# First layer of a two-layer kernel: chunk 1 loaded in halves, ten matmuls on zeros, and padded rows for the first batch's mask, W and x

## The chip, the cores and the metric

The kernel runs on one core of one Trainium2 chip. The metric is the device time of one execution in microseconds (us), lower is better. A core has TensorE (PE; its weight loads are shown as PEld), VectorE (DVE), ScalarE (ACT), GpSimd (POOL) and SyncE (SP), which here only issues transfers. Sixteen DMA engines move data between the chip's memory (HBM) and the on-chip memory.

## The reference, cut to what matters

There are 8 batches of 256 rows and 1024 features, all in float32. Two layers follow each other, each with a residual:

```python
# layer 0, for each batch b
y = x[b] + x[b] @ W.T + bias + coeff[b] * (x[b] @ (2 * mask[b] - 1))
# layer 1
out[b] = y + y @ weight[ids[b]].T
```

mask is (8, 1024, 1024) of int32 zeros and ones, W is (1024, 1024), weight is (8, 1024, 1024), and ids picks one of the 8 weights for each batch.

## The kernel before, in words

**Layer 0 as one product.** The mask of a batch is turned into a weight: ScalarE computes 2c * mask - c in place ("scale"), VectorE adds W transposed ("fold"), and TensorE multiplies x by the result. Layer 1 multiplies y by the chosen weight.

**Stages.** There are 16 stages: layer 0 and layer 1 of 8 batches. All but the first are computed as a two by two block product with seven block multiplications (p1 to p7, in the order p1, p5, p6, p2, p7, p3, p4) instead of eight. That costs VectorE sums of blocks of x (s1 to s4, line L542) and of weight blocks (t1 to t4, line L559). In this first block stage, which is layer 1 of batch 0, t1 is block 12 minus 11, t2 is 22 minus t1, t3 is 22 minus 12, and t4 is 21 minus t2. p5 needs s1 and t1, p6 needs s2 and t2, p7 needs s3 and t3. Its matmuls are L598; those of all later stages are L608. Results are gathered by L672.

**The first stage is done plainly**, because everything waits for the first data. Its 1024 input features are 8 chunks of 128 (k = 0 to 7). A chunk has a mask row block (`mask0`, loaded on L283), a W row block (`w0T`, L287, into `w0_sb`) and a slice of x (`x0T`, L274). A whole chunk of mask or of W is 128 partitions by 1024 numbers, 512 KB. The list `pieces` holds what is loaded at once: before, chunk 0 in two halves of 512 columns and chunks 1 to 7 whole. Each piece has a load of the mask, a load of W, a scale (`scale_first`, ACT L301), a fold (`fold_first`, DVE L309) and its matmuls (`mm_first`, PE L316: two records of the profile to one call, 16 to a chunk). `parts` cuts scale and fold of a piece into smaller instructions: the first piece by 256 columns and piece 2, which is chunk 1, by 512. x comes in three loads that `load_w0` issues behind pieces 0, 2 and 3: for chunks 0 and 1 (256 KB), 2 and 3 (256 KB) and 4 to 7 (512 KB). The results are evicted with bias and residual by `evict_first` (DVE L343), in four instructions, two for each half of the outputs.

**The order.** Work is described as tasks with an engine, an estimated length, their inputs and a latest time. `plan` simulates the engines with these estimates and emits tasks by planned start, so each engine's order is fixed at build time and each engine then runs strictly in its order. All loads are issued by SP in one queue. The framework gives DMAs eight completion semaphores in rotation, so a load is not issued before the one eight places ahead of it has landed; the coefficients' load, issued by ACT, takes the first of them. Weight and mask buffers (11 of 1 MB) come free when their last user is done.

**Before the first data.** TensorE runs eight matmuls of bfloat16 zeros, 512 columns each (L806), and among them, after the fifth, one that spreads the 8 coefficients over all partitions (L808). VectorE makes the two scale factors from it (L809, L810), and ScalarE's first scale waits for them.

Of the kernel before, what the change touches and what calls it, by code (L numbers as in the profile page):

```python
# [14 lines left out]
P = 128  # L15
Q = 32
BLOCKS = ("11", "12", "22", "21")
WBUFS = 11


PRODUCTS = {
# [120 lines left out]
def kernel(  # L142
# [26 lines left out]
    nc = tc.nc  # L169
    B = coeff.shape[1]  # L170
    _, _, _, KH, TH = xT.shape
    NL, _, _, _, H = w1T.shape
    KC, D = 2 * KH, 2 * H
# [4 lines left out]
        for name, bufs in (  # L178
            ("const", 1),
            ("w", WBUFS),  # L180
            ("a", 3),
# [8 lines left out]
    )  # L190
    room = {"w": WBUFS, "a": 3, "r": 3, "turn": 2, "s1": 2, "u2": 2, "ps": 8}
    shapes = {
# [16 lines left out]
    zeros = const.tile([P, H], BF16, name="zeros")  # L209
# [10 lines left out]
    def task(*args, **kw):  # L220
        tasks.append(Task(*args, **kw))
        return tasks[-1]

    def take(r: Buffer):
        count[0] += 1
        r.tile = pools[r.pool].tile(shapes[r.pool], F32, tag=r.pool, name=f"{r.pool}_{count[0]}")
        return r.tile
# [30 lines left out]
    first = {(j, h): Buffer("ps") for j in range(2) for h in range(2)}  # L258
    xb = Buffer("r")
    half = KH // 2  # L260
    pieces = [(0, ds(0, H)), (0, ds(H, H))] + [(k, ds(0, D)) for k in range(1, KC)]
    w0_rows = w0_sb.rearrange("p k j n -> p k (j n)")

    def x0_view():
        flat = x0.tile.rearrange("p q k n -> p (q k n)")[:, 0 : KC * 2 * TH]
        return flat.rearrange("p (k n) -> p k n", k=KC)
# [5 lines left out]
    def load_x0(lo: int, hi: int, queue):  # L272
        pairs = slice(lo // 2, hi // 2)
        queue.dma_start(  # L274
            out=x0_view()[:, lo:hi].rearrange("p (g k) n -> p g (k n)", k=2),
            in_=x0T[pairs].rearrange("g p n -> p g n"),
        )

    def load_mask(n: int):
        k, cols = pieces[n]  # L280
        if m[k // 2].tile is None:
            take(m[k // 2])
        nc.sync.dma_start(out=m_view(k)[:, cols].bitcast(I32), in_=mask0[k][:, cols])  # L283

    def load_w0(n: int):
        k, cols = pieces[n]
        nc.sync.dma_start(out=w0_rows[:, k, cols], in_=w0T[k][:, cols])  # L287
        if n in (0, 2, 3):
            load_x0(*{0: (0, 2), 2: (2, KH), 3: (KH, KC)}[n], nc.sync)

    def parts(n: int):

        k, cols = pieces[n]
        size = {0: 2 * P, 2: H}.get(n, cols.size)
        return k, [ds(at, size) for at in range(cols.start, cols.start + cols.size, size)]

    def scale_first(n: int):
        k, spans = parts(n)
        for cols in spans:
            t = m_view(k)[:, cols]  # L300
            nc.scalar.activation(  # L301
                t, t.bitcast(I32), AF.Identity, bias=cn_sb[:, 0:1], scale=c2_sb[:, 0:1]
            )

    def fold_first(n: int):
        k, spans = parts(n)
        for cols in spans:
            t = m_view(k)[:, cols]
            v.tensor_tensor(t, t, w0_rows[:, k, cols], ALU.add)  # L309
# [43 lines left out]
    for n, (k, cols) in enumerate(pieces):  # L353
        share = cols.size / D
        opens = opened != k // 2
        length = {0: 0.4, 2: 0.75}.get(n, 1.22 * share)
        ld = task(
            "DMA",
            1.32 * share,
            lambda n=n: load_mask(n),  # L360
            takes=[m[k // 2]] if opens else [],
            uses=[] if opens else [m[k // 2]],
            latency=1.5,
            latest=0.2 * n,
        )
        ld2 = task(
            "DMA", 1.32 * share, lambda n=n: load_w0(n), latency=1.5, latest=0.2 * n + 0.1
        )
        sc = task("ACT", length, lambda n=n: scale_first(n), after=[ld], uses=[m[k // 2]])
        fo = task("DVE", length, lambda n=n: fold_first(n), after=[sc, ld2], uses=[m[k // 2]])  # L370
        folded.append(fo)
        last_scale = sc
        opened = k // 2
        if n == 0:
            tasks[0].takes = [x0] + list(tasks[0].takes)
            tasks[0].uses = [x0] + list(tasks[0].uses)
            x0.users += 1
# [91 lines left out]
    def stage(s: int):  # L469
# [66 lines left out]
        def sum_of(what: str, after=()):  # L536
# [24 lines left out]
            for n, rows in enumerate(parts):  # L561
                t = task(
                    "DVE",
                    BLOCK / len(parts),
                    lambda rows=rows: emit(rows),
                    after=[done[left], done[right], done.get(what), *after],
                    takes=[W[what]] if fresh and n == 0 else [],
                    uses=src + ([W[what]] if fresh and n else []),
                )
                if fresh and n == 0:  # L570
                    t.stage = s
                done[what] = t
# [222 lines left out]
    with tc.manual_schedule():  # L795
        take(x0)
        nc.scalar.dma_start(out=c_row, in_=coeff)
        v.memset(zeros, 0.0)
        v.memset(ones, 1.0)
        v.memset(warm, 0.0)  # L800

        nc.scalar.activation(warm, warm, AF.Identity, bias=warm, scale=1.0)
        idle = pools["ps"].tile([P, H], F32, tag="ps", name="idle")
        c_ps = pools["ps"].tile([P, B], F32, tag="ps", name="c_ps")
        for n in range(8):
            nc.tensor.matmul(out=idle, lhsT=zeros[:, 0:P], rhs=zeros, start=True, stop=True)  # L806
            if n == 4:
                nc.tensor.matmul(out=c_ps, lhsT=ones, rhs=c_row, start=True, stop=True)  # L808
                v.tensor_scalar(c2_sb, c_ps, 2.0, None, ALU.mult)  # L809
                v.tensor_scalar(cn_sb, c_ps, -1.0, None, ALU.mult)  # L810
        for t in plan(tasks, room, may_take):
            t.emit()
            if t is folded[0]:

                v.memset(ids_sb, 0)
                v.memset(b_sb, 0.0)
                nc.gpsimd.dma_start(out=ids_sb, in_=ids)
                nc.gpsimd.dma_start(out=b_sb, in_=biasT)
# [58 lines left out]
```

## Time and profile before

| what | value |
|---|---|
| time, three runs | 403.77, 404.0, 405.08 us; median 404.0 |
| profiled execution | 404.47 us, span from the first to the last instruction 402.7 us |
| TensorE busy | 396.5 us, 98% of the span, 1154 records |
| VectorE busy | 330.5 us, 82% |
| ScalarE busy | 183.5 us, 46% |
| GpSimd busy | 27.2 us, 7% |
| moved by DMA | 102.99 MB, mean 256 GB/s; by SP's queue 87.23 MB |
| granted TensorE clock | 0.999 |

How to read the profile's lines. A line of the groups or the timeline names the engine, the source line, the operation, output and input tiles, shapes and count; in brackets stands how long the engine was idle before and what ended the wait. In the timeline the first number is the start in us from the span's start and the second the length. In the windows view each row is a stretch of time with the busy time of each engine asked for and, in brackets, its count of instructions, then the granted clock, the DMA engines' busy share and GB/s. In the list of waits, each line tells who waited for whom: total us, times, longest. In the chain, each step is followed back to what released it.

### The profile page before, as it was taken

What the parts mean: (1) busy time and instruction counts of PE and PEld (TensorE: products, weight loads), DVE (VectorE), ACT (ScalarE), POOL (GpSimd) and SP (SyncE); (2) the same over time, 40 slices, a digit from 0 to 9 for tenths busy, and PEclk for the clock granted to TensorE, in tenths of its full rate; (3) what the DMA queues carried; (4) which work ended last, traced back from release to release, by engine and by line L of the source; (5) the groups of instructions that cost most, each with busy time, mean ns of one, the idle gap of its engine ahead of it and who ended that gap; (6) DMA issues with size and microseconds to landing.
All of it is one profiled execution on the core that took longest, in us unless ns stands there. A gap on an engine that the chain in (4) does not pass through costs nothing.

```text
span 402.7 us, 3428 instructions
## 1 busy us (share of the span) xinstructions
PE 396.5 (98%) x1154; PEld 201.8 (50%) x1154; DVE 330.5 (82%) x306; ACT 183.5 (46%) x303; POOL 27.2 (7%) x44
## 2 busy tenths in 40 slices
PE   8899999999999999999999999999999999999996
PEld 5689995444444444444444444444444444444443
DVE  2347999999999999799968998789977999668242
ACT  3461735205952396880069610894119920391000
POOL 1000111100011100011010100102001020001101
PEclk9999999999999999999999999999999999999999
DMA  7999999982696828958399583987659694701102
GB/s 268 408 413 422 422 335 400 380 293 107 251 343 194 357 104 341 335 164 319 111 401 304 187 336 112 370 255 282 239 200 338 194 365 157 281 33 53 53 0 105
DMA packets 18564, 102.99 MB, mean 256 GB/s; under 512 B 2226, under 2 KB 2482, under 8 KB 9074
## 3 DMA queue, kind: packets, MB, share of 16 engines
q1 hardware_dynamic: 13952, 87.23, 55.9%
q0 software_dynamic: 4448, 15.47, 14.4%
q8 instruction: 9, 0.15, 0.1%
q14 instruction: 9, 0.07, 0.1%
q10 hardware_dynamic: 146, 0.07, 0.1%
HBM read 94.38 MB, written 8.39 MB: 255 GB/s over the span
## 4 chain that ended last, share of the span: by engine, by line
PE 92%; DMA 4%; DVE 2%; issue 1%; SPq 0%; DVEq 0%
PE ps L608 84%; PE ps L598 5%; DMA w_sb<-w0T 4%; PE ps L316 4%; DVE w L559 1%; DVE a L343 0%; DVE w L309 0%; SPq L283 0%; DVE a L542 0%; SPq L274 0%; SPq L287 0%; DVE r L757 0%; DVEq L343 0%; DVEq L309 0%
## 5 line engine op out<-in xcount | busy, mean ns | idle before, releaser
L608 PE MATMUL ps<-w,a 128*128 128x512 f32 (+1 forms) x792 | 336.7, 588 | 0.0
L608 PEld LDWEIGHTS ps<-w,a 128*128 128x128 f32 x792 | 149.9, 190 | 186.7 <-issue 183.4
L559 DVE TENSOR_TENSOR w<-w,w 128x2048 f32<-128x2048 f32 (+1 forms) x61 | 136.8, 2252 | 3.0 <-PE ps L608 2.5
L453 ACT ACTIVATE a<-turn 32x256 f32<-32x256 f32 x224 | 92.7, 414 | 68.5 <-DVE turn L439 65.7
L672 DVE TENSOR_TENSOR r<-r,ps 128x512 f32<-128x512 f32 x73 | 49.1, 680 | 24.9 <-PE ps L608 24.6
L529 DVE TENSOR_TENSOR w<-w,w_sb 128x2048 f32<-128x2048 f32 x28 | 63.9, 2286 | 5.7 <-ACT w L515 5.7
L515 ACT ACTIVATE w<-w,cn_sb,c_sb 128x2048 f32<-128x2048 int32 x28 | 58.5, 2091 | 15.7 <-DMA w<-mask 15.3
L542 DVE TENSOR_TENSOR a<-a 128x512 f32<-128x512 f32 x59 | 39.4, 686 | 0.3
L644 ACT ACTIVATE s<-ps 128x512 f32<-128x512 f32 x15 | 8.9, 591 | 63.2 <-PE ps L608 54.0
L316 PE MATMUL ps<-a,w 128*128 128x256 f32 x128 | 30.5, 399 | 1.1 <-DVE w L309 1.0
L698 POOL DMA_DIRECT2D out<-r x31 | 17.0, 550 | 190.1 <-DVE r L672 190.0
L316 PEld LDWEIGHTS ps<-a,w 128*128 128x128 f32 x128 | 25.3, 201 | 6.8 <-DVE w L309 3.2
L644 ACT ACTIVATE u<-ps 128x512 f32<-128x512 f32 x15 | 8.9, 595 | 39.2 <-PE ps L608 38.8
L309 DVE TENSOR_TENSOR w<-w,w_sb 128x1024 f32<-128x1024 f32 (+2 forms) x11 | 10.2, 934 | 15.2 <-DMA w_sb<-w0T 12.8
L598 PE MATMUL ps<-a,w 128*128 128x128 f32 x192 | 22.0, 276 | 0.2 <-DVE a L542 0.2
L598 PEld LDWEIGHTS ps<-a,w 128*128 128x128 f32 x192 | 21.8, 192 | 0.5 <-DVE a L542 0.4
L418 POOL DMA_DIRECT2D r<-bias x7 | 8.7, 1245 | 173.9 <-DMA r<-xR 173.9
L439 DVE STREAM_TRANSPOSE turn<-r 128x512 f32<-128x512 f32 x28 | 19.8, 708 | 0.6
L301 ACT ACTIVATE w<-w,cn_sb,c_sb 128x1024 f32<-128x1024 int32 (+2 forms) x11 | 10.9, 1004 | 14.6 <-DMA w<-mask 13.1
L672 DVE TENSOR_TENSOR r<-r,s 128x512 f32<-128x512 f32 x14 | 9.6, 684 | 6.6 <-ACT s L644 6.6
L672 DVE TENSOR_TENSOR r<-r,u 128x512 f32<-128x512 f32 x14 | 9.6, 686 | 3.4 <-ACT u L644 3.4
L343 DVE TENSOR_TENSOR a<-ps,r 128x512 f32<-128x512 f32 x4 | 2.7, 688 | 3.2 <-PE ps L316 3.2
(27 smaller groups left out, 24.8 us busy)
## 6 DMA issues: line engine op xcount, KB each, us to landing
w<-w1T SPq DMA_DIRECT2D x32, 1024.0 KB, 8.4
w<-mask SPq DMA_DIRECT2D x28, 1024.0 KB, 10.0
out<-r POOLq DMA_DIRECT2D x31, 256.0 KB, 7.4
r<-xR SPq DMA_DIRECT2D x7, 1024.0 KB, 8.0
a<-xT SPq DMA_DIRECT2D x7, 1024.0 KB, 9.2
r<-bias POOLq DMA_DIRECT2D x7, 1024.0 KB, 15.7
w<-mask SPq DMA_DIRECT2D x7, 512.0 KB, 9.9
w_sb<-w0T SPq DMA_DIRECT2D x7, 512.0 KB, 10.2
```

Source lines behind the costliest of these rows:

```text
L316: nc.tensor.matmul(out=t.rearrange("p (c n) -> p c n", c=half)[:, c % half], lhsT=m_view(k)[:, ts(oc, P)], rhs=x0_view()[:, k], start=k == ...
L439: lambda t=t, opens=not turned: v.transpose(out=(take(r) if opens else r.tile)[:, t], in_=view(source.tile)[:, 2 * t + j]),
L453: nc.scalar.activation(to[:, :, :, f], src[:, :, :, g], AF.Copy)
L515: nc.scalar.activation(t, t.bitcast(I32), AF.Identity, bias=cn_sb[:, b : b + 1], scale=c2_sb[:, b : b + 1])
L529: lambda q=q: v.tensor_tensor(W[q].tile, W[q].tile, w0[q], ALU.add),
L542: lambda: v.tensor_tensor(part(what), part(left), part(right), op),
L559: v.tensor_tensor(to[:, rows], a, c, op)
L598: nc.tensor.matmul(out=t[:, ts(c, TH)], lhsT=W[w].tile[:, k, ts(c, P)], rhs=part(a)[:, k], start=opens and c == 0 and k == 0, stop=k == KH ...
L608: nc.tensor.matmul(out=t[:, cols], lhsT=part(a)[:, k], rhs=W[w].tile[:, k, cols], start=opens and k == 0, stop=k == KH - 1, skip_group_che ...
L644: lambda: nc.scalar.activation(take(r), bank.tile, AF.Copy),
L672: v.tensor_tensor(to, left, get(r), op)
L698: lambda: (queue or nc.gpsimd).dma_start(out=out0[:, block(q)] if flipped else out[b - 1, :, int(q[0]) - 1, lo:hi], in_=R[b].tile[:, block ...
```

## The change

Five things change.

- `pieces`: chunk 1 is loaded, scaled and folded in two halves of 512 columns, as chunk 0 already is. There are now ten pieces, and chunks 2 to 7 are pieces 4 to 9.
- The loads of x follow pieces 0, 3 and 5: the second still comes behind chunk 1, and the third behind chunk 3 instead of chunk 2.
- `parts`, and the planner's length of it: the split of scale and fold into 512 columns goes from chunk 1, which is now halved anyway, to chunk 2.
- The zeros: after the eight matmuls of 512 columns come one of 256 and one of 128.
- `PAD`: each row of `w0T`, `x0T` and `mask0` in HBM gets 128 unused numbers (512 bytes) at its end. Rows of mask and W lie 4608 bytes apart instead of 4096, rows of x 2560 instead of 2048. The loads read the same numbers as before.

The planner runs with the new tasks, so the order changes elsewhere too. On SP only the loads named here differ up to the first weights. On VectorE, in the first block stage, t3 moves from before the last two evictions to behind s2 and one L672 sum; one weight fold of the next stage moves back by two instructions; and in later stages some weight sums, one s sum and two transposes move by a few places. Lines of the tile function from L277 on are two higher than before (L316 becomes L318, L598 L600), and those at the end a little more.

```diff
+PAD = 128
...
-    pieces = [(0, ds(0, H)), (0, ds(H, H))] + [(k, ds(0, D)) for k in range(1, KC)]
+    pieces = [(k, ds(j * H, H)) for k in range(2) for j in range(2)]
+    pieces += [(k, ds(0, D)) for k in range(2, KC)]
...
-            in_=x0T[pairs].rearrange("g p n -> p g n"),
+            in_=x0T[pairs, :, 0 : 4 * TH].rearrange("g p n -> p g n"),
...
         nc.sync.dma_start(out=w0_rows[:, k, cols], in_=w0T[k][:, cols])
-        if n in (0, 2, 3):
-            load_x0(*{0: (0, 2), 2: (2, KH), 3: (KH, KC)}[n], nc.sync)
+        if n in (0, 3, 5):
+            load_x0(*{0: (0, 2), 3: (2, KH), 5: (KH, KC)}[n], nc.sync)
...
-        size = {0: 2 * P, 2: H}.get(n, cols.size)
+        size = {0: 2 * P, 4: H}.get(n, cols.size)
...
-        length = {0: 0.4, 2: 0.75}.get(n, 1.22 * share)
+        length = {0: 0.4, 4: 0.75}.get(n, 1.22 * share)
...
-        for n in range(8):
-            nc.tensor.matmul(out=idle, lhsT=zeros[:, 0:P], rhs=zeros, start=True, stop=True)
+        for n, size in enumerate((H, H, H, H, H, H, H, H, 2 * P, P)):
+            nc.tensor.matmul(
+                out=idle[:, 0:size], lhsT=zeros[:, 0:P], rhs=zeros[:, 0:size], start=True, stop=True
+            )
...
+    for k in ("w0T", "x0T", "mask0"):
+        arrays[k] = np.pad(arrays[k], ((0, 0), (0, 0), (0, PAD)))
```

## The prediction, made before the changed kernel ran

> **What bounds the kernel now.** I read the chain of work that ended last, then what TensorE waited for, then TensorE's first 45 us in order of time, then the stretch that fills its gaps. The chain's shares and all of TensorE's waits:
>
> ```profile
> PE 92%; DMA 4%; DVE 2%; issue 1%; SPq 0%; DVEq 0%
> PE idle L806 <- DVE zeros L798: 1.2, 1, 1.2
> PE ps L316 <- DVE w L309: 1.0, 2, 0.8
> PE ps L598 <- DVE a L542: 0.2, 1, 0.2
> ```
>
> TensorE is the bound, and what it waits for lies in the first 41 us. From 40.83 on it has no gap, so a microsecond won before that is won at the end, if nobody else falls behind. The timeline of TensorE (start, length):
>
> ```profile
> 3.97 1.46 PE L806 MATMUL idle<-zeros 128*128 128x512 bf16 x3
> 5.49 5.54 PE L316 MATMUL ps<-a,w 128*128 128x256 f32 x16
> 11.81 7.50 PE L316 MATMUL ps<-a,w 128*128 128x256 f32 x32 [0.78 <-DVE w L309]
> 19.50 17.53 PE L316 MATMUL ps<-a,w 128*128 128x256 f32 x80 [0.19 <-DVE w L309]
> 36.87 3.73 PE L598 MATMUL ps<-a,w 128*128 128x128 f32 x32
> 40.83 4.40 PE L598 MATMUL ps<-a,w 128*128 128x128 f32 x37 [0.22 <-DVE a L542]
> ```
>
> A chunk is 16 records of L316. At full rate starts are 0.2155 us apart, so a chunk is 3.45; chunks 1 to 7 need 24.1 us. Chunk 0 begins at 5.49, chunk 1 at 11.81, 2 at 15.58, 3 at 19.50, and from there 80 records run without a wait to the next line at 36.87. The gaps shown understate the loss: they are counted after a modelled matmul end. By starts, chunk 3 comes 7.69 after chunk 1, where 6.90 would do. What feeds them, in the timelines of VectorE and ScalarE:
>
> ```profile
> 9.67 1.52 ACT L301 ACTIVATE w<-w,cn_sb,c_sb 128x512 f32<-128x512 int32 x2 [2.01 <-DMA w<-mask]
> 11.06 1.29 DVE L309 TENSOR_TENSOR w<-w,w_sb 128x512 f32<-128x512 f32 x2 [2.68 <-DMA w_sb<-w0T]
> 14.30 1.23 DVE L309 TENSOR_TENSOR w<-w,w_sb 128x1024 f32<-128x1024 f32 x1 [1.95 <-DMA w_sb<-w0T]
> 18.22 1.23 DVE L309 TENSOR_TENSOR w<-w,w_sb 128x1024 f32<-128x1024 f32 x1 [2.69 <-DMA w_sb<-w0T]
> 20.78 1.23 DVE L309 TENSOR_TENSOR w<-w,w_sb 128x1024 f32<-128x1024 f32 x1 [1.34 <-DMA w_sb<-w0T]
> ```
>
> Each fold waits for W's chunk. Chunk 3 arrives 3.9 us after chunk 2, later ones every 2.56: between them lie the 512 KB of x that load_w0 issues. From chunk 3 on arrivals outrun TensorE. The last stall is VectorE's own order:
>
> ```profile
> 32.82 0.69 DVE L343 TENSOR_TENSOR a<-ps,r 128x512 f32<-128x512 f32 x1 [3.03 <-PE ps L316]
> 34.29 4.55 DVE L559 TENSOR_TENSOR w<-w,w 128x1024 f32<-128x1024 f32 x3
> 38.76 1.28 DVE L343 TENSOR_TENSOR a<-ps,r 128x512 f32<-128x512 f32 x2
> 40.08 0.69 DVE L542 TENSOR_TENSOR a<-a 128x512 f32<-128x512 f32 x1
> ```
>
> The evictions at 38.76 could have started at 37; they stand behind a 2.29 us weight sum (t3, the third of the L559 row). s1 at 40.08 comes late and p5 starts at 40.83. By starts, p1 to p6 takes 7.63 us (36.87 to 44.50) where two products at 3.57 need 7.14: 0.49 lost.
>
> **Chunk 1 in halves.** The same bytes come as four loads of 256 KB instead of two of 512. The 1 MB of chunk 1 now lands half by 9.2 (midway between W's landings, 7.47 and 10.94). The first half's mask is there near 8.5, its scaling 0.81 puts it at 9.3, and the fold of 0.69 ends at 10.1. TensorE ends chunk 0 at 10.87 (last start 10.65 plus 0.22), so chunk 1 starts there, not at 11.81. The second half folds from about 11.2 to 11.9 (landing near 11.07, 0.69); TensorE wants it at 12.6. Chunk 1 is done at 14.3 to 14.4. The two added loads cost SP 0.42 us each while queued bytes cover it. SP's order now makes load 8 wait for the coefficients and 9 for the first mask (landed at 3.39); later waits are for loads in order, with over 2 MB issued ahead, so I cost the queue at nothing. Without that cover a late issue would cost its 0.42.
>
> 2 KB packets take 84 ns each in the trace's packet records, 4 KB ones 159 to 164: 32 x 84 against 16 x 160 ns per engine is 0.13 us later for everything behind.
>
> **What moves with the halves.** Chunk 2 takes over the split into 512 columns: W at 14.3 + 0.13, one fold of 0.69 instead of 1.23, so TensorE starts it at 15.17 instead of 15.58. It waits 0.8 there, and a first matmul after a wait costs 0.1 more. The 512 KB of x moves behind chunk 3, which lands 1.28 earlier: fold from 17.07 to 18.3, wanted at 18.75. So it no longer waits. Chunk 4 is where it was, plus 0.13: folded at 22.13, wanted at 22.2; x is there at 18.3. Hence 15.2 + 0.1 + 96 x 0.2155 = 35.99 for p1's start, against 36.87: **0.88 us**.
>
> The plan changes too. On VectorE t3 goes behind the evictions, s1, t2, s2 and one L672. With chunk 7 ended at 36.0, the two evictions (0.65 each in a row) and s1 end at 38.0, and p5 is wanted at 39.6: no stall, **0.49 us** more. t2 then ends at 40.3, s2 at 40.9 (p6 wants them at 43.1), t3 at 43.7 and s3 at 45 (p7 wants them at 50.3). Other moves after 60 us shift single weight sums or transposes by one or two places; in the trace the products they feed have 2.1 us to spare or more.
>
> **Zeros.** The last 512-wide one streams until 5.22; the new 256 and 128 columns at the half rate (0.213, 0.107) run to 5.54, so they fill the gap and delay the first real matmul by up to 0.08. Chunk 1's end moves to 14.4, under the 15.17 of chunk 2: nothing. On the clock, the windows of L316 (length, busy, count):
>
> ```profile
> 5.50:9.00 3.50, 3.50 (x8) 1.00 1.01 356
> 9.40:11.00 1.60, 1.60 (x8) 1.00 1.08 409
> ```
>
> Eight in 3.5 us, then eight in 1.6: starts are 0.427 apart until 9.04 and 0.2155 after 9.35, though the granted clock reads 1.00 throughout. The Trainium skill (TensorE: Matmul & The Clock Gate, Part 1) says half rate ends after about 3.4 us of sustained activity, in a free-running window. By the row it took 8 us from 1.20, with breaks at 3.3 to 4.0 (the coefficient matmul) and 5.2 to 5.5. By the rule, one break fewer may bring full rate at about 5.8, ending chunk 0 up to 1.7 earlier; but chunk 1's half is not there before 10.1 and chunk 2 not before 15.17, so by either the sum is unchanged. If full rate comes only at 11.9, chunk 0 ends at 12.3 and the 0.88 falls to about 0.2.
>
> **Rows 512 bytes longer.** Nothing in the trace shows it, so it is bounded. For a gain: the rates by window (last column GB/s) are
>
> ```profile
> 4.00:5.00 1.00, 1.00 (x4) 0.25 (x3) 0.26 (x3) 0.65 (x2) 0.00 (x0) 1.00 0.94 231
> 9.00:10.00 1.00, 1.00 (x5) 0.86 (x4) 0.00 (x0) 0.33 (x1) 0.00 (x0) 1.00 1.04 410
> 18.00:19.00 1.00, 1.00 (x7) 0.80 (x5) 0.78 (x1) 0.11 (x1) 0.00 (x0) 1.00 1.06 422
> ```
>
> Between 2 and 9 us packets take up to 1.65 us instead of 84 or 160 ns; that excess adds up to 1.0 us per engine, the most padding can win. Against it, full rows at the same pitch of 4 KB run at 401 to 422 GB/s from 9 on, and the slow packets include rows that lie end to end. The skill (DMA: Bandwidth & Descriptors, Latency and other measured facts) reports slow copies at power-of-two row pitches, but from 512 KB up, cured by 4 KB more and not by 192 bytes: by that rule a 512 byte pad at a pitch of 4 KB need not help. For a loss: chunks no longer lie in one piece; if the disturbed rate of the early windows became usual, a fifth (my estimate, 410 to 330 GB/s). I take zero, the row of the undisturbed packets.
>
> **Sum.** 0.88 + 0.49 = 1.37 us. The profiled execution took 404.47 (span 402.7, 1.77 around it), so 403.1; the median of the runs shown lies 0.47 lower: **402.6**.
>
> **VectorE as cover.** It is busy from 40 to 160 us but for 1.6. It waits once, 0.91 at 68.5 to 69.44, for p5 of the next stage. Its work from 34.29 to 68.53 is 34.24 us; starting when the weights land (33.45 + 0.13) it ends at 67.8, p5 at 67.9: it keeps pace. p1 of the stage at 110.44 needs ScalarE's turns, done at 109.42: 1.0 in hand.
>
> **Rivals.**
> A (0.42): as summed, 402.6; its own range 402.1 to 403.2.
> B (0.26), padding takes the early excess away: loads 1.0 earlier; chunk 2 starts at 14.4, when chunk 1 ends, and no chunk waits: 14.4 + 96 x 0.2155 = 35.1, gain 1.78 + 0.49 = 2.27: 401.7. For: the early windows. Against: the end-to-end rows.
> C (0.16), the gain is mostly hidden: chunk 4's fold later than 22.2, a late full rate, or VectorE behind at 110: 0.2 to 0.9 won, 403.4.
> D (0.16), slower: padded rows load slower. It decides at chunk 4: about 6.3 MB lie ahead of its fold, 15.4 us at 410 GB/s. At 9% slower (1.4 us) the gain is gone. At 20%, chunk 4 is folded at 25.2 to 25.9, up to 2.8 after its start now (23.1), and t1's weights come later still, so the 0.49 goes too: about 406.5. For: loads bound this stretch. Against: the packet durations of 9 us on look engine-bound, not memory-bound.
>
> **Numbers.** About 0.3% (1.2 us) is what a measurement of this kernel can tell from no change. A lies just beyond it: 0.62 of it is faster, the rest same. Faster 0.42 x 0.62 + 0.26 = 0.52; same 0.16 + 0.16 = 0.32; slower 0.16. From B's best (401.4) to the lower part of D (405.2), the range leaves out about 0.15.
>
> **What would show it.** Right: L318 (L316 before) with one wait near 15, none at 11.8 or 19.5; p1 (now L600) at 36.0; no wait for s1. B: 350 GB/s or more in the windows at 3 to 7. D: 4 KB packets over 175 ns, chunk 4's fold after 23.5. I am wrong if p1 starts after 36.6, or if a wait appears after 60.

## The result, and the profile after

| | before | changed |
|---|---|---|
| median of the runs | 404.2 us (403.77 to 405.08, 7 runs) | 402.53 us (401.9 to 402.92, 7 runs) |
| profiled execution | 404.47 us, span 402.7 | 402.53 us, span 400.8 |
| p1 starts (first block product) | 36.87 | 35.80 |
| p6 starts | 44.50 | 42.95 |

The ratio of the means is 0.9953, with an interval of 0.9942 to 0.9965. By medians that is 1.67 us less, by means 1.91, where 1.37 had been forecast (402.6).

The chain of work that ended last, as the changed kernel's page sums it by engine:

```profile
PE 95%; DMA 3%; SPq 0%; DVE 0%; issue 0%; DVEq 0%
```

TensorE's waits in the changed kernel (what it waited for and what ended the wait; total us, count, longest):

```profile
PE idle L808 <- DVE zeros L800: 1.2, 1, 1.2
PE ps L318 <- DVE b_sb L820: 0.3, 1, 0.3
```

VectorE's steps (a fold, the evictions, s1) are nearly gone from the chain. The waits for folds and for s1 are gone from the list; a new one of 0.3 stands ahead of the first real matmul. (The view names a setting of `b_sb` for it; the load of x landed at 5.93, just before the start at 6.06.) TensorE's timeline:

```profile
3.97 1.78 PE L808 MATMUL idle<-zeros 128*128 128x512 bf16 x5
6.06 29.90 PE L318 MATMUL ps<-a,w 128*128 128x256 f32 x128 [0.31 <-DVE b_sb L820]
35.80 9.43 PE L600 MATMUL ps<-a,w 128*128 128x128 f32 x83
```

The whole first stage is one row: 128 records with no wait that this view can show, and the block products join it without one. Looking at single starts, one short wait is left: chunk 1's last record starts at 14.48 and chunk 2's first at 14.90. From p6 on every product starts 1.55 or 1.56 us earlier than before, to the last stage; the remaining 0.35 of the difference in span lies behind the last matmul. There the last store lands 2.40 us after the start of that matmul instead of 2.62, and the program ends 1.16 after the landing instead of 1.29. So nothing was given back after 45 us, and 0.35 was won at a place that the forecast did not look at. VectorE, with what it waited for:

```profile
14.16 1.29 DVE L311 TENSOR_TENSOR w<-w,w_sb 128x512 f32<-128x512 f32 x2 [2.55 <-DMA w_sb<-w0T]
16.69 1.23 DVE L311 TENSOR_TENSOR w<-w,w_sb 128x1024 f32<-128x1024 f32 x1 [1.24 <-DMA w_sb<-w0T]
20.61 1.22 DVE L311 TENSOR_TENSOR w<-w,w_sb 128x1024 f32<-128x1024 f32 x1 [2.69 <-DMA w_sb<-w0T]
...
32.62 0.69 DVE L345 TENSOR_TENSOR a<-ps,r 128x512 f32<-128x512 f32 x1 [0.17 <-PE ps L318]
33.91 2.36 DVE L561 TENSOR_TENSOR w<-w,w 128x1024 f32<-128x1024 f32 x2 [0.60 <-DMA w<-w1T]
36.19 1.28 DVE L345 TENSOR_TENSOR a<-ps,r 128x512 f32<-128x512 f32 x2
37.51 0.69 DVE L544 TENSOR_TENSOR a<-a 128x512 f32<-128x512 f32 x1
38.12 2.28 DVE L561 TENSOR_TENSOR w<-w,w 128x2048 f32<-128x2048 f32 x1
```

Chunk 3 is folded at 16.69 instead of 18.22, and the long gap between arrivals has moved behind it, to chunk 4 (20.61), where TensorE still has work. The evictions at 36.19 follow t1 at once, s1 ends at 38.2, and p5, which wants it at 39.37, finds it there. The L561 row at 38.12 is t2.

The early loads look as before (windows of one us; last two columns the DMA engines' busy share and GB/s):

```profile
4.00:5.00 1.00, 1.00 (x4) 0.40 (x4) 0.25 (x3) 0.65 (x2) 0.00 (x0) 1.00 0.85 246
9.00:10.00 1.00, 1.00 (x5) 0.83 (x5) 0.42 (x1) 0.54 (x1) 0.00 (x0) 1.00 1.04 402
```

The packets' excess over 84 and 160 ns, per engine up to 10 us, is 1.2 us; before it was 1.1. So this one profile shows no effect of the padding on the early loads. The times of the experiments below say that the padding is worth something.

### The profile page after: what moved, and what is told of

Its sections match the earlier page's. It is cut to its first block, busy times and chain, and to the rows that moved or that the text cites. A ratio compares the mean times of both kernels' runs of the same rounds, so it can differ in the third digit from the quotient of the medians.

```text
span 400.8 us, 3435 instructions
## 1 busy us (share of the span) xinstructions
PE 395.9 (99%) x1156; PEld 201.9 (50%) x1156; DVE 330.7 (83%) x307; ACT 183.9 (46%) x304; POOL 27.2 (7%) x44
## 4 chain that ended last, share of the span: by engine, by line
PE 95%; DMA 3%; SPq 0%; DVE 0%; issue 0%; DVEq 0%
PE ps L610 84%; PE ps L600 6%; PE ps L318 5%; DMA w_sb<-w0T 2%; DMA w<-mask 1%; DVE w L311 0%; SPq L276 0%; SPq L289 0%; SPq L285 0%; DVE r L759 0%; DVEq L311 0%
## 5 line engine op out<-in xcount | busy, mean ns | idle before, releaser
L561 DVE TENSOR_TENSOR w<-w,w 128x2048 f32<-128x2048 f32 (+1 forms) x61 | 136.6, 2249 | 3.1 <-PE ps L610 2.1
L517 ACT ACTIVATE w<-w,cn_sb,c_sb 128x2048 f32<-128x2048 int32 x28 | 58.5, 2091 | 14.4 <-DMA w<-mask 13.6
L318 PE MATMUL ps<-a,w 128*128 128x256 f32 x128 | 29.9, 396 | 0.4 <-DVE b_sb L820 0.3
L318 PEld LDWEIGHTS ps<-a,w 128*128 128x128 f32 x128 | 25.3, 199 | 4.9 <-DVE b_sb L820 0.7
L311 DVE TENSOR_TENSOR w<-w,w_sb 128x512 f32<-128x512 f32 (+2 forms) x12 | 10.3, 869 | 15.5 <-DMA w_sb<-w0T 11.3
L600 PE MATMUL ps<-a,w 128*128 128x128 f32 x192 | 21.8, 275 | 0.0
L600 PEld LDWEIGHTS ps<-a,w 128*128 128x128 f32 x192 | 21.7, 192 | 0.1
L303 ACT ACTIVATE w<-w,cn_sb,c_sb 128x512 f32<-128x512 int32 (+2 forms) x12 | 11.2, 953 | 14.9 <-DMA w<-mask 13.4
L808 PE MATMUL idle<-zeros 128*128 128x512 bf16 (+2 forms) x10 | 4.1, 575 | 1.2 <-DVE zeros L800 1.2
```

Of the source, the lines that this page charges most:

```text
L318: nc.tensor.matmul(out=t.rearrange("p (c n) -> p c n", c=half)[:, c % half], lhsT=m_view(k)[:, ts(oc, P)], rhs=x0_view()[:, k], start=k == ...
L517: nc.scalar.activation(t, t.bitcast(I32), AF.Identity, bias=cn_sb[:, b : b + 1], scale=c2_sb[:, b : b + 1])
L561: v.tensor_tensor(to[:, rows], a, c, op)
L600: nc.tensor.matmul(out=t[:, ts(c, TH)], lhsT=W[w].tile[:, k, ts(c, P)], rhs=part(a)[:, k], start=opens and c == 0 and k == 0, stop=k == KH ...
```

## Experiments

Theory to start with: the order of the loads and the order of VectorE make the whole gain; padding and zeros make none. Rivals: padding speeds the loads; the zeros speed the clock; the halves alone are enough. Where means are given they are over the timed runs of one kernel, beside 404.4 to 404.7 for the kernel before (404.40, 404.50 and 404.70 on the three chips of these experiments).

### Padding alone

```diff
+    for k in ("w0T", "x0T", "mask0"):
+        arrays[k] = np.pad(arrays[k], ((0, 0), (0, 0), (0, PAD)))
```

> The kernel before with the 512 bytes of padding alone. My theory: padding does nothing; the packets' excess of 1.0 us per engine in the first 9 us stays, chunk 3 starts at 19.5, p1 at 36.9, p6 at 44.5, and the time is the kernel before's (404.2, ratio 1.000). Rival (padding helps the early loads): excess under 0.4, 350 GB/s or more between 3 and 7 us, chunk 3 up to 0.9 earlier (18.6), time 403.3 or less. Rival (padding hurts): 4 KB packets over 170 ns and p1 after 37.2.

Measured: ratio 0.9991 (0.9983 to 0.9999), mean of 14 runs 404.05. p1 at 36.82, p6 at 44.46, chunk 3 at 19.45, excess 1.5 us. Up to the last matmul the profile is the kernel before's; the time is about 0.3 lower, just beyond its interval. Neither form of the padding rival shows in the early loads. But the span is 0.23 shorter, and 0.18 of that lies at the other end: the last store, issued by ACT, lands sooner after its issue. For the kernel before and then this one:

```profile
DMA to landing us min/median/max: 2.0/2.0/2.0
DMA to landing us min/median/max: 1.8/1.8/1.8
```

This holds for all 14 profiles: counted from the start of the last matmul, that store lands after 2.56 to 2.62 us in the six without padding and after 2.38 to 2.44 in the eight with it, though its packets are through at 1.87 to 1.89 in every one. Why is not shown; only input arrays are padded, and padding x alone is enough. What is left of the 0.3 for the loads is within the noise.

### The changed kernel without padding

```diff
-    for k in ("w0T", "x0T", "mask0"):
-        arrays[k] = np.pad(arrays[k], ((0, 0), (0, 0), (0, PAD)))
```

> The changed kernel with the rows at their old pitch. My theory: the same as the changed kernel, 402.5 (ratio to the kernel before 0.9955), p1 between 35.8 and 36.0, p6 at 43.0 to 43.1. Rival (half rows at a pitch of 4 KB need the padding): more slow 2 KB packets between 4 and 9 us, chunk 2 starts 0.5 to 1 later than 14.9, p1 at 36.4 or later, time 403.1 or more.

Measured: ratio 0.9964 (0.9951 to 0.9977), median 402.82, runs from 402.64 to 403.69. The profiled execution was the slowest of them (403.69): the first load of x landed at 7.29, TensorE began only at 7.42, and p1 came at 36.79. Two things follow. In this execution a late first x went straight to the end, for no wait was left behind it; with the loads of before, a first matmul at 6.80 (see the next experiment) cost nothing, but TensorE ran at full rate from there, so the two cannot be compared cleanly. And padding may be worth something: the rival's mark for p1 (36.4 or later) was met, its mark for slow packets was not (excess 1.2, as with padding), and the median lies between the two forecasts. This was taken up again below.

### The order of VectorE alone

The kernel before, with t3 put behind t2, which reproduces VectorE's order of the changed kernel from the evictions on:

```diff
-            sum_of("t3")
+            sum_of("t3", [done["t2"]])
```

> The kernel before with one thing: t3 of the first block stage is made to wait for t2, which gives VectorE the order of the changed kernel from the evictions on; loads, halves, zeros and pitch as before. My theory: p1 stays at 36.9, the last evictions start at 37.0, s1 ends near 39.0, p5 starts at 40.4 without a wait and p6 at 44.0: 0.5 us less, 403.7 (ratio 0.9988). Rival (the time won at s1 is given back, because t3 and what follows it come later): p6 at 44.0, but a wait after 44.5 and 404.2.

Measured: ratio 0.999 (0.9983 to 0.9997), 403.62. VectorE's timeline (start, busy, instruction; in brackets the wait ahead of it):

```profile
34.21 2.36 DVE L559 TENSOR_TENSOR w<-w,w 128x1024 f32<-128x1024 f32 x2 [0.17 <-DMA w<-w1T]
36.49 1.28 DVE L343 TENSOR_TENSOR a<-ps,r 128x512 f32<-128x512 f32 x2
37.81 0.69 DVE L542 TENSOR_TENSOR a<-a 128x512 f32<-128x512 f32 x1
```

The evictions follow t1 at once, and s1 the evictions, ahead of t3. TensorE's timeline in the same kernel:

```profile
19.16 17.53 PE L316 MATMUL ps<-a,w 128*128 128x256 f32 x80 [0.18 <-DVE w L309]
36.53 8.65 PE L598 MATMUL ps<-a,w 128*128 128x128 f32 x76
```

L598 is one row: p5 at 40.10 follows p1 without a wait, 7.14 from p1 to p6 against 7.63. The 0.5 us of the forecast is there, in the trace and about so in the time (0.57 by means), and nothing takes it back later. (p1 itself is 0.3 earlier because this execution's loads were.)

### The order undone in the changed kernel

```diff
+                    earliest=HOLD if j else 0.0,   # HOLD = 38.0, on the last two evictions
```

> The changed kernel with the last two evictions held in the plan until 38 us, which puts t3 before them again, as in the kernel before; loads, halves, zeros and padding stay. My theory: p1 at 35.8 as in the changed kernel, t3 from 36.2 to 38.5, evictions to 39.8, s1 to 40.5, so p5 starts at 40.55 instead of 39.4: 1.2 us more than the changed kernel, 403.7, so the earlier loads alone are worth only about 0.5. Rival (the terms add up as in the forecast, the order being worth 0.5 in any setting): 403.0.

Measured: ratio 0.9978 (0.9972 to 0.9984), 403.6. TensorE's timeline:

```profile
35.44 3.73 PE L601 MATMUL ps<-a,w 128*128 128x128 f32 x32
40.34 3.84 PE L601 MATMUL ps<-a,w 128*128 128x128 f32 x32 [1.17 <-DVE a L545]
```

VectorE's timeline in the same kernel:

```profile
33.65 4.71 DVE L562 TENSOR_TENSOR w<-w,w 128x1024 f32<-128x1024 f32 x3 [0.70 <-DMA w<-w1T]
38.28 1.28 DVE L346 TENSOR_TENSOR a<-ps,r 128x512 f32<-128x512 f32 x2
39.59 0.69 DVE L545 TENSOR_TENSOR a<-a 128x512 f32<-128x512 f32 x1
```

The first stage ends earlier than ever, and TensorE then waits 1.17 us for s1, because t1 and t3 hang on the weights' landing (33.65) and not on TensorE. From p1 to p6 it takes 8.58 us instead of 7.15. VectorE's order differs in later stages too, but from p6 to the last matmul both kernels take 354.26 us, so that costs nothing. The rival, that the two terms add up in any setting, is out: with early loads the order is worth about 1.2 (403.66 against 402.41 by means), without them 0.5. The order alone brings 0.6 by means, the early loads with the padding 0.7, and all together 1.9.

### x later, alone

```diff
-        if n in (0, 2, 3):
-            load_x0(*{0: (0, 2), 2: (2, KH), 3: (KH, KC)}[n], nc.sync)
+        if n in (0, 2, 4):
+            load_x0(*{0: (0, 2), 2: (2, KH), 4: (KH, KC)}[n], nc.sync)
```

> The kernel before with one thing: the 512 KB of x for chunks 4 to 7 is issued behind chunk 3 instead of chunk 2. The engines' orders are otherwise those of the kernel before. My theory: chunk 2 still starts at 15.6, chunk 3 is folded by 18.2 and starts without a wait at 19.1, p1 at 36.5, p6 at 44.1: 0.4 us less, 403.9 (ratio 0.9991). Rival (chunk 4 becomes the late one, as its x now lands last): a wait at chunk 4 and p1 at 36.9, 404.3.

Measured: ratio 0.9995 (0.9985 to 1.0005). In the profile the wait ahead of chunk 3 is gone and chunk 4 has none, with p1 at 36.15 and p6 at 43.85, but W of chunk 2 also landed 0.25 earlier there than in the kernel before. The time doesn't tell 0.4 from nothing: inconclusive, with the rival (a wait at chunk 4) out.

### The changed kernel with x where it was

```diff
-        if n in (0, 3, 5):
-            load_x0(*{0: (0, 2), 3: (2, KH), 5: (KH, KC)}[n], nc.sync)
+        if n in (0, 3, 4):
+            load_x0(*{0: (0, 2), 3: (2, KH), 4: (KH, KC)}[n], nc.sync)
```

> The changed kernel with one thing undone: the 512 KB of x is issued behind chunk 2 again; halves, split of chunk 2, order of VectorE, zeros and padding stay. My theory: chunks 1 and 2 start early as in the changed kernel (11.2 and 14.9), but chunk 3 is folded only at 19.2 and waits, p1 at 36.6, p6 at 43.8, time 403.6 (ratio 0.9984): halves alone are worth next to nothing before chunk 3, and with them only the order of VectorE counts. Rival (halves are the main gain): p1 at 36.1 or earlier and 402.9.

Measured: ratio 0.996 (0.9946 to 0.9975), 402.89, where 403.6 was expected. TensorE's timeline:

```profile
14.19 3.72 PE L318 MATMUL ps<-a,w 128*128 128x256 f32 x16 [0.44 <-DVE w L311]
18.61 17.53 PE L318 MATMUL ps<-a,w 128*128 128x256 f32 x80 [0.70 <-DVE w L311]
35.98 9.21 PE L600 MATMUL ps<-a,w 128*128 128x128 f32 x81
```

Chunk 3 waits as expected, 0.70. But it waits until 18.61 and not 19.2: W of chunk 2 landed at 13.32 in this execution, W of chunk 3 at 17.23, against 14.21 and 18.12 in the kernel before, though the same bytes stood ahead of them. So the rival's marks were met (p1 at 36.1 or earlier, 402.9), and the theory that the halves (here with the padding) are worth next to nothing without the later x is out. Moving x later is worth about 0.4 on top (402.90 against 402.48 by means, give or take 0.3, for the next kernel, which has it and two matmuls on zeros less, on the same chip). Whether the earlier landing is the padding's, the halves' or chance is not shown.

### Eight matmuls on zeros

```diff
-        for n, size in enumerate((H, H, H, H, H, H, H, H, 2 * P, P)):
+        for n, size in enumerate((H, H, H, H, H, H, H, H)):
```

> The changed kernel with the eight matmuls on zeros of before, without the two short ones. My theory: full rate comes at the same place, near 9.2, p1 at 35.5 to 36.1 and the time is the changed kernel's, 402.5 (ratio 0.9955). Rival (the short ones keep the clock on its way): full rate later than 9.6, by up to 3 us, which delays chunk 1's end by up to 1.3 and p1 to 36.5 or later, 403.1 or more.

Measured: ratio 0.9948 (0.9933 to 0.9964), 402.6: the changed kernel's time, as far as the runs can tell. The windows of its first stage (length, busy, count):

```profile
6.00:10.00 4.00, 4.00 (x10) 1.00 1.04 376
10.70:14.00 3.30, 3.30 (x17) 1.00 1.02 394
```

Ten records in 4 us are starts 0.43 apart: half rate until 10.4. That looks like the rival, but the changed kernel with x where it was, which has ten, shows in its windows full rate from the first matmul on:

```profile
6.00:8.00 2.00, 1.94 (x8) 1.00 1.02 346
```

Over all 14 profiles full rate was there from the first real matmul in 3 of 5 kernels with eight zeros, and in 3 of 9 with ten; the others ran at half rate until 9.0 to 10.5. The two short matmuls don't decide it.

### Only x padded

```diff
-    for k in ("w0T", "x0T", "mask0"):
+    for k in ("x0T",):
```

> The changed kernel with only x's rows padded; mask and W at their old pitch. The profiles so far have x's first load landing at 5.8 to 6.1 with padding (three kernels) and at 5.4 to 7.3 without (three). My theory: chance, 402.5 to 402.8 with x landing anywhere in 5.4 to 7.3. Rival 1 (the padding of x spares x a straggler): x lands at 5.7 to 6.2 and the time is 402.5. Rival 2 (mask and W are what the padding helps): 402.9 or more.

Measured: ratio 0.996 (0.9944 to 0.9975), median 402.96, with x's first load landing at 5.85. x came in time and yet the time was not 402.5, which is the second rival's mark. But what this execution lost, it lost late. TensorE's timeline:

```profile
30.80 5.45 PE L318 MATMUL ps<-a,w 128*128 128x256 f32 x24 [0.31 <-DVE w L311]
```

Chunk 7's mask landed 2.82 us after the load ahead of it, where 1.28 is usual (see the last section), and TensorE waited for its fold: 0.57 by starts, so p1 came at 36.09 and not at 35.52. The early loads of this profile are as good as with full padding (W of chunk 2 at 13.76). The intervals overlap those of both neighbours; which tensor counts stays open.

### Padding again, on one chip

The changed kernel and the one without padding, run beside each other:

> The changed kernel again, beside the next one on the same chip: 402.5.

> The changed kernel with the rows at their old pitch, again, beside it. Padding is worth 0.3 to 0.6: 402.8 to 403.1, x's first load landing after 6.1 in most runs. Padding is worth nothing: 402.5, and the difference of the first time was chance.

Measured: 402.29 with padding (0.9938, 0.9924 to 0.9951), 402.91 without (0.9956, 0.9941 to 0.9972). Means 402.31 and 403.00. With the earlier runs that is 402.41 over 13 runs against 403.03 over 11; from their spread the difference is 0.62 us, give or take 0.33. A third pair follows with the same sign. The two profiles of this pair differ by 0.28 in span: 0.16 at the last store, as above, and 0.12 at p1, because x landed at 6.26 instead of 6.46. In neither does TensorE wait between its first real matmul and p1. With padding:

```profile
6.39 29.77 PE L318 MATMUL ps<-a,w 128*128 128x256 f32 x128 [0.64 <-DMA a<-x0T]
36.00 9.21 PE L600 MATMUL ps<-a,w 128*128 128x128 f32 x81
```

So in this second profile of the changed kernel, with half rate until 9.9, TensorE itself is the bound from 6.39 on, and not the landing of chunk 2.

### x as it is needed, with and without padding

The experiments point to two things that still cost: the first x, and what lies ahead of chunk 2's W. So:

```diff
-        if n in (0, 3, 5):
-            load_x0(*{0: (0, 2), 3: (2, KH), 5: (KH, KC)}[n], nc.sync)
+        if n < 2:
+            nc.sync.dma_start(out=x0_view()[:, n], in_=x0T[0][:, ds(n * 2 * TH, 2 * TH)])
+        elif n in (4, 6):
+            load_x0(*{4: (2, KH), 6: (KH, KC)}[n], nc.sync)
```

> The changed kernel with x loaded as it is needed: chunk 0's 128 KB behind the first half of chunk 0, chunk 1's behind the second half, chunks 2 and 3 behind chunk 2's W, chunks 4 to 7 behind chunk 4's W; the engines' other orders stay. My theory: what bounds the changed kernel now is the landing of the first x (TensorE starts at 6.0) and chunk 2's W; here TensorE starts at 5.5 to 5.6, chunk 2's W lands 0.6 earlier, p1 at 34.6 to 35.2, nothing later gets in the way, 401.6 (ratio to the kernel before 0.993). Rival (VectorE, without idle from 40 to 160 us, becomes the bound, since t1 still waits for weights that land at 33.8): p1 as early, but a wait of TensorE at p5 or near 109 us, and 402.2 or more.

> The same with the rows at their old pitch. After eight kernels the padding looks like more than nothing: means of the runs are 404.05 with it alone against 404.40, and 402.5 with it against 403.1 in the changed kernel. Padding is worth 0.3 to 0.6: 402.0 to 402.2 here, and runs spread more widely. Padding is worth nothing: 401.6, as with it.

Measured: 402.32 with padding (0.9938, 0.9925 to 0.9951), 402.86 without (0.9953, 0.9939 to 0.9966). It doesn't beat the changed kernel beside it (402.29). The waits of the padded one:

```profile
PE idle L810 <- DVE zeros L802: 1.2, 1, 1.2
PE ps L320 <- DVE b_sb L822: 0.2, 1, 0.2
```

The theory failed on its first step, and the rival's late wait is not there either. Half of the bytes didn't land earlier: chunk 0's 128 KB of x landed at 5.79, as the 256 KB did at 5.8 to 6.3 in the other kernels with padded x. TensorE began at 5.93 and ran to p1 at 35.89 with no wait that the view shows: 29.96 us, of which 128 x 0.2155 = 27.6 is full rate; 0.14 by starts is lost ahead of chunk 7, and the rest is half rate until about 10. In that execution TensorE was the bound almost throughout, from its first real matmul on, and earlier W could not have helped. The pair gives the padding 0.54 by medians. Its two profiles put that elsewhere than in the first loads: TensorE began at 5.93 and 5.96, W of chunk 2 landed at 13.60 and 13.58, and the 0.50 between their p1 arises at chunk 7, behind a load that came late in both, by 0.5 more without padding (see the last section).

## Why the prediction was right, and where a term was off

The two terms that made up the forecast, the earlier loads and the order of VectorE, are there at about their sizes. That the time came within 0.1 us of 402.6 is in part luck: the gain was larger than forecast, and the kernel before, taken at 404.0 from three runs, had a median of 404.2 in seven. Chunk 2 as the one wait that is left is in part luck too. Of the ten profiles with halves, four wait there (the changed kernel's first, and the three that had full rate from the first real matmul); in the other six TensorE, at half rate until 9.5 to 10.5, came so late that it did not wait for chunk 2 at all.

- *Chunk 1 in halves, x moved*: p1 was forecast at 35.99, 0.88 earlier, and came at 35.80, 1.07 earlier. Chunk 1 followed chunk 0 without a gap (11.24, forecast 10.9, later because TensorE began at 6.06 and not at 5.5), chunk 2 was the one that still waited (14.90, forecast 15.2), chunks 3 and 4 did not. The late start was just absorbed: of the forecast's slack ahead of chunk 2, 0.2 was left. In the second profile of the same kernel nothing was left, and p1 came at 36.00. No run has the halves alone; their share of this term is read from the timelines.
- *The 0.13 us for 2 KB packets* did not show: W of chunk 2 landed at 14.04, where 14.21 + 0.13 = 14.34 was forecast; that landing scatters by more than this.
- *The order of VectorE*: forecast 0.49, measured 0.48 to 0.49 (7.15 from p1 to p6 against 7.63), shown alone by the order put into the kernel before. What the forecast didn't see is that the order is worth 1.2 once the first stage is early, so the parts do not simply add: the early loads without it keep 0.5 in the trace.
- *Zeros*: costed at nothing, and the runs cannot tell it from nothing.
- *Rows 512 bytes longer*: this is the step that was mis-sized. The forecast took zero of a range from 1.0 down, by the undisturbed packets of 9 us on and by the rule of the Trainium skill (DMA: Bandwidth & Descriptors, Latency and other measured facts). That rule's own figures begin at far larger pitches than 4 KB, and slow copies stand there from 2 MB up; at 512 KB it has 207 GB/s against 214 for a padded pitch. Measured in pairs, padding is worth 0.5 to 0.7 with the halves, and about 0.3 in the kernel before. The forecast looked for it in the loads only; 0.16 to 0.19 of it stands at the last store in every pair of profiles. The rest, about 0.45 give or take 0.33, has no one place in the traces: it is the landing of the first x in two pairs and a late load at chunk 7 in the third. W of chunk 2 lands at 13.3 to 14.0 in five profiles with halves and full padding, at 14.1 and 14.6 in two without, but at 13.6 either way in the pair with x as it is needed. The excess of slow packets, which the forecast took as the padding's measure, is 1.0 to 1.2 with it and 1.2 to 1.3 without in those seven profiles, and once, in the last kernel without padding, 0.4. So the cause stays open.
- Without padding the changed kernel's ratios, 0.9964 and 0.9956, are 1.45 to 1.8 us: the forecast's other terms came to 1.37, and about 0.2 is the end of the program. With padding the means gave 1.9, and 2.4 in the later comparison.
- *VectorE as cover*: no wait of TensorE appeared after 45 us, though VectorE is busy for 118.6 of the 120 us from 40 to 160.
- The rival by which padded rows load slower is out. The one by which the padding takes all of the early excess away is out as well by its own mark (293, 246, 279 and 293 GB/s in the windows from 3 to 7 us), though padding does have a worth.

## What to carry to other kernels

When the data of a first stage arrive in pieces, look for the piece that comes latest against its use, and count by starts, not by the gaps that a modelled end leaves: here chunk 3 stood behind x that nobody needed for another 7 us. A stage that ends earlier pays only if the engines behind it are ready in that order; check what stands ahead of the hand-over in each queue, since the same reordering was worth 0.5 us before and 1.2 after. And an effect of half a microsecond in loads that scatter by as much is not seen in one profile: run pairs on one chip before calling it nothing, and compare the profiles to their last instruction before saying where it lies.

## What the runs showed of the hardware that was not expected

- TensorE's rate in the first 10 us differs from execution to execution, whatever was run on zeros before: starts 0.2155 us apart from the first real matmul on in 6 of 14 profiles, 0.427 apart until 9.0 to 10.5 in the other 8. The granted clock reads 1.00 either way. The rule of the Trainium skill weighed in the prediction (TensorE: Matmul & The Clock Gate, Part 1: about 3.4 us of sustained activity, in a window that runs freely) fits if one counts from the first real matmul: half rate lasted 3.1 to 4.4 us from there in those 8. That would mean that the zeros, with their breaks, counted for nothing in these executions and for enough in the other 6; no run here tests it.
- A packet of 16 KB on an instruction queue, at 24.4 to 26.1 us in all 14 profiles, takes 1.1 us. In 13 of them one of the loads that land from 26 to 29 us comes 1.4 to 2.8 us after the load ahead of it, instead of 1.28 (chunk 7's mask 2.10 in the changed kernel). That the packet delays that load is read from their order in time; it is not shown. Where the loads had less in hand, TensorE waited for it: in the kernel with only x padded, above, and with x as needed and no padding, by 0.81 by starts:

```profile
31.10 5.45 PE L320 MATMUL ps<-a,w 128*128 128x256 f32 x24 [0.55 <-DVE w L313]
```

- The landing of x's first load sets TensorE's start, which comes 0.13 to 0.14 us later, and scatters: 5.8 to 6.3 us in seven profiles with x padded and 256 KB, 5.4 to 7.3 in five without padding.
